# Attention with top-1 experts on one core: rows of the next sequence loaded and stored by tiles of 128 tokens, steps behind a block's end two halves later

## The chip, the core and the metric

The kernel runs on one core of a Trainium2 chip. The metric is the device time of one execution in microseconds; the time before is the median of three executions. All times below are microseconds unless a row says ns. In the profile PE is TensorE's matmuls, PEld its weight loads, DVE is VectorE, ACT ScalarE, POOL GpSimd and SP SyncE. GpSimd and SyncE each issue transfers on a queue of their own.

## What is computed

Four sequences of 2048 tokens with 512 features are normalised (layer norm), go through 16-head attention with a spectral filter on queries and keys, and through a top-1 router with eight experts of capacity 100 that share one weight matrix. Cut to what matters:

```python
xn = _layernorm(x)                                   # x: 4 x 2048 x 512
q, k, v = split(xn @ w_qkv)                          # 16 heads of 32
q, k = _spectral_filter(q, mask), _spectral_filter(k, mask)
attn = softmax(einsum('bhqd,bhkd->bhqk', q, k) / sqrt(dh))
a = einsum('bhqk,bhkd->bhqd', attn, v).reshape(B, S, D) @ w_out + b_out
f = combine @ (dispatched @ w_expert + b_expert)     # first 100 tokens of each expert
out = x + a + f
```

## The kernel before

**Tiling.** Four sequences `b`, four groups of four heads `c` in each: `k = 4 b + c` runs from 0 to 15. The queries of a group come in four blocks `n` of 512 (`QB`); a block goes over 16 key tiles of 128. Handling one key tile `j` is called a **half**, two halves are a **window**. A block has `HB` = 16 halves, a group `GH` = 64, the kernel 1024, numbered through. "Half 46 of k = 2" below is counted from that group's start.

**A half on the engines.** TensorE writes the negated row maxima into four banks of the accumulator (`negm` with `ones_b`), adds the scores (`k,q`), and between them computes scores the other way round (`q,k`) for the maxima of a later block, which VectorE reduces (`part`). ScalarE takes four exponentials into a tile called `even` or `odd`. TensorE multiplies the tile of the half before with the values, and VectorE adds the product to `num`. The accumulator `array` has eight banks, taken in turn.

**Row sums.** The tiles of a window are added by an accumulating transfer on GpSimd's queue (`even<-odd`, 1 MB, `pair`), one window later. Another window later GpSimd adds the sum of the window before to it (`add_to`, two operations of 128x1024), and waits for the transfer to land. There are five `even` tiles and three `odd` ones.

**Order.** Each engine works in program order. In each window the loop of the last lines of the kernel emits: `max_split` of a block whose maxima are complete, the entries of `heads` (a block's `divide`), the `pair` of the window before, the `add_to` of two windows before, and then for each half the matmuls and exponentials and the steps that stand in `agenda` for it. SyncE's transfers are in program order too, but an issue starts as soon as what it waits for is there, so it may run far ahead of its half.

**What ends a block.** `close_steps` (line 654) places, counted in halves from the block's end, `fold` at 5, eight `invert` at 6 to 13, `divide` in `heads` at 14 (it writes `ot` on GpSimd), four `result` (a projection of `ot` on TensorE and a copy to `y` on ScalarE) from 15 to 18, and `add` at 19: `y` is added to the output in memory, 1 MB on GpSimd's queue. So `divide` belongs to the last window of the following block. In the same window `max_split` (line 162) makes three rows of the next block's maxima on GpSimd (`rest`, `row`), and three small transfers on SyncE's queue bring them to `negm`, which the next block's first matmuls read.

**A change of sequence.** In group c = 2 of each of the first three sequences (k = 2, 6, 10) `plan` (line 862) places the first pass over the next sequence's rows: `load` of a chunk of 512 tokens (1 MB, `xs`, two buffers), `measure` (mean and variance on VectorE), `bias` (adds `b_out` on GpSimd), `first_sums` (stores the chunk to the output), `scale` (four small operations on GpSimd that turn 16 variances into factors). Then the rows are loaded again for normalising and transposing in group c = 3. The entries of `in_stage` are numbers into the tuple that `token_stage` returns: 0 load, 1 measure, 2 scale, 3 normalize, 4 turn, 5 route, 6 bias, 7 first_sums. The first sequence is measured and normalised before the loop; only its `bias` and `first_sums` are placed, in k = 0.

```python
            for n, (come, go) in enumerate(((22, 38), (30, 46), (40, 56), (48, GH))):
                at(start + come, in_stage, 0, n)
                at(start + go, in_stage, 7, n)
            for i in range(NT):
                at(start + 26 + 2 * i + 2 * (i // 8), in_stage, 1, i)
                at(start + 28 + 2 * i + 2 * (i // 8), in_stage, 6, i)
            at(start + GH - 4, in_stage, 2)
```

**Experts.** `place_experts` (line 844) gathers the experts' rows in k = 12; `gather_row`, `add_row` and `scatter_row` add them to the output in k = 13 and 14, one tile in each block.

Projections of the next group are spread over a group by `spread`, which fills halves evenly with regard to the `cost` that other steps have put there.

Of the kernel before, what the change touches and what calls it, by code (L numbers as in the profile page):

```python
# [26 lines left out]
NT = S // P  # L27
# [4 lines left out]
NQ = S // QB  # L32
TQ = QB // P
# [69 lines left out]
def attention_and_top1_experts(ctx: ExitStack, tc: tile.TileContext, a: dict, out: bass.AP):  # L103
    nc = tc.nc
    x = a["L0_attn_x"].rearrange("b (g t p) d -> b g p t d", t=TQ, p=P)
    o = out.rearrange("b (g t p) d -> b g p t d", t=TQ, p=P)
# [50 lines left out]
    def chunk(name):  # L157
        tag, bufs = ("y", 1) if name == "y" else ("xs", None)
        return chunks.tile([P, TQ, DM], F32, tag=tag, name=name, bufs=bufs)
# [25 lines left out]
    on = SimpleNamespace(sync=nc.sync)  # L185
# [36 lines left out]
    def token_stage(b):  # L222
# [4 lines left out]
        held = {}  # L227

        def load(n, tile=None):
            held[n] = chunk("xs") if tile is None else tile  # L230
            on.sync.dma_start(out=held[n], in_=x[b, n])

        def measure(i):
            on.vector.bn_stats(stats[:, i, :], held[i // TQ][:, i % TQ, :])
            on.vector.bn_aggr(mv[:, i, :], stats[:, i, :])
# [2 lines left out]
            row = held[i // TQ][:, i % TQ, :]  # L238
            on.gpsimd.tensor_tensor(row, row, b_out, ALU.add)

        def first_sums(n):

            on.sync.dma_start(out=o[b, n], in_=held[n])

        def scale(first=0, last=NT, shift_on=None):
            at = slice(first, last)
# [52 lines left out]
        first = small.tile([P, NT], F32, name="first")  # L299
# [78 lines left out]
        def enter(i):  # L378
            on.gpsimd.indirect_dma_start(
                tables[i % NTAB],  # L380
                bass.IndirectOffsetOnAxis(ap=slot[:, i : i + 1], axis=0),
                entry[:, i, :],
                None,
                bounds_check=SLOTS - 1,
                oob_is_err=False,
            )

        route = [score, by_token, below_top, exponentials, divide, best, ranked, first_best, place, carry_on, locate, note]
        route += [lambda i=i: enter(i) for i in range(NT)]
        return load, measure, scale, normalize, turn, route, bias, first_sums  # L390


    qs, ks, vs = {}, {}, {}
# [249 lines left out]
    def row_sums(tiles):  # L643
        pf = bank()
        for tile in tiles:
            four_heads(pf, lambda at: ones[:, 0:DH], tile, start=tile is tiles[0], stop=tile is tiles[-1])
        return pf

    def project(k, ot, t):
        pj = bank()  # L650
        columns(pj, ot[:, t * P : (t + 1) * P], wo[k], start=True, stop=True)
        return pj

    def close_steps(k, n):

        b = k // NG
        held = {}

        def fold():
            held["den"] = work.tile([P, QB], F32, tag="den", name="den", bufs=1)  # L660
            held["factor"] = work.tile([P, QB], F32, tag="factor", name="factor", bufs=1)
            on.scalar.copy(held["den"], row_sums([ended[k, n][1]]))

        def invert(i):
            at = slice(i * PART, (i + 1) * PART)
            on.vector.reciprocal(held["factor"][:, at], held["den"][:, at])

        def divide():
            held["ot"] = work.tile([P, QB], F32, tag="ot", name="ot", bufs=1)
            on.gpsimd.tensor_tensor(held["ot"], ended[k, n][0], held["factor"], ALU.mult)  # L670

        def result(t):
            if t == 0:
                held["y"] = chunk("y")
            on.scalar.copy(held["y"][:, t, :], project(k, held["ot"], t))

        def add():
            on.gpsimd.dma_start(out=o[b, n], in_=held["y"], accum_op=ALU.add)

        if (k, n) == (B * NG - 1, NQ - 2):  # L680
            steps = [(7, 1, fold)] + [(8 + i // 2, 0, invert, i) for i in range(QB // PART)]
            first = 12
        else:
            steps = [(5, 1, fold)] + [(6 + i, 0, invert, i) for i in range(QB // PART)]
            first = 15
        steps += [(first + t, 1, result, t) for t in range(TQ)]
        return steps + [(first + TQ - 1 + first % 2, 0, add)], (first - first % 2, divide)

    def close_last(k, n, num, tiles, y):

# [11 lines left out]
                on.sync.dma_start(out=o[b, n, :, t - 1 : t + 1, :], in_=y[:, t - 1 : t + 1, :])  # L702


    load, measure, scale, normalize, turn, first_route, first_bias, first_sums = token_stage(0)

    load(0)
    load(1)
# [8 lines left out]
    turned, filtered = ([f[2 * s + i] for f in filters for s in range(2)] for i in range(2))  # L717
# [57 lines left out]
    for i, item in enumerate(stream[:MAX_AHEAD]):  # L775
# [4 lines left out]
        half = next(turns), next(turns)  # L780
# [12 lines left out]
    HB = NT  # L793
    GH = NQ * HB
# [6 lines left out]
    def at(half, step, *args, cost=0):  # L801
        agenda[half].append(lambda: step(*args))
        costs[half] += cost
# [28 lines left out]
    def in_stage(which, *args):  # L832
        stage["all"][which](*args)
# [4 lines left out]
    def plan_route(first, step):  # L838

        costs_of = {0: NR, 1: 1, 7: 3}  # L840
        for i in range(ROUTE):
            at(first + 2 * i, step, i, cost=costs_of.get(i, 0))

    def place_experts(start):


        begin, fetch, measure, scale, expert = expert_steps()
        first = start + 36
        at(first, begin)
        for i in range(ST):  # L850
            at(first + 2 + 2 * i, fetch, i)
            at(first + 6 + 2 * i, measure, i)
        at(first + 22, scale)
        for i in range(ST + 2):
            at(first + 26 + 2 * i, expert, i, cost=(NR if i >= 2 else 0) + (1 if 1 <= i <= ST else 0))
        for i in range(ST):
            free = start + GH + i * HB + 22
            for step in (gather_row, add_row, scatter_row):
                at(free, step, i)
                free += 2  # L860

    def plan(k):

        b, c = divmod(k, NG)
        start = k * GH
        if k == 0:
            for n in range(NQ):
                at(2 + 8 * n, load, n)
                for i in range(TQ):
                    at(6 + 8 * n + i, first_bias, n * TQ + i)  # L870
                at(12 + 8 * n, first_sums, n)
        if k + 1 == B * NG:
            return
        at(start + GH // 2, load_out_weights, k + 1)
        last = start + GH - 4
        steps = []
        if k == 0:
            done = spread([(1, 0, step) for step in first_projections], 15)
            at(done[-1] + 1, load_qkv_weights, 1)
            plan_route(20, lambda i: first_route[i]())  # L880
            ready = done[-1] + 3
        if c == NG - 2 and b + 1 < B:

            at(start + 20, begin_stage, b + 1)
            for n, (come, go) in enumerate(((22, 38), (30, 46), (40, 56), (48, GH))):
                at(start + come, in_stage, 0, n)
                at(start + go, in_stage, 7, n)
            for i in range(NT):
                at(start + 26 + 2 * i + 2 * (i // 8), in_stage, 1, i)
                at(start + 28 + 2 * i + 2 * (i // 8), in_stage, 6, i)  # L890
            at(start + GH - 4, in_stage, 2)
            at(start + GH - 4, in_stage, 0, 0)
            at(start + GH + 2, in_stage, 0, 1)
        pieces = projections(k + 1)
        if c == NG - 1:

            late = {8: 9, 12: 14}
            order = [("turn", i) for i in range(8)] + pieces[:4] + [("turn", i) for i in range(8, 12)]
            order += pieces[4:8] + [("turn", i) for i in range(12, NT)] + pieces[8:]
            steps, first = [], start + 1  # L900
            for step in order:
                if isinstance(step, tuple):
                    i = step[1]
                    steps.append((1, start + late[i] if i in late else 0, lambda i=i: in_stage(4, i)))
                else:
                    steps.append((1, 0, step))
            steps[0] = (1, first, steps[0][2])
            done = spread(steps, last)
            turned = {i: done[order.index(("turn", i))] for i in range(NT)}
            for i in range(NT):  # L910
                at(turned[i] - 1, in_stage, 3, i)
            for n in (2, 3):
                at(turned[4 * n - 5] + 1, in_stage, 0, n)
            plan_route(turned[NT - 1] + 2, follow_route)
        else:
            done = spread([(1, ready if k == 0 else start, step) for step in pieces], last)
        assert done[-4] >= start + 3 * HB and done[-8] >= start + 2 * HB
        if k + 2 < B * NG:
            at(done[-1] + 1, load_qkv_weights, k + 2)
# [12 lines left out]
    for block in range(1, B * NG * NQ):  # L932

        costs[block * HB - 4] += 0.5
    place_experts((B - 1) * NG * GH)
    for k in range(B * NG):
        plan(k)
# [12 lines left out]
    for k in range(B * NG):  # L950
        for n in range(NQ):
            num = work.tile([P, QB], F32, tag="num", name="num")
            tiles = {}
            for w in range(NW):
# [9 lines left out]
                for j in (even, odd):  # L964
# [5 lines left out]
                    for u in range(2):  # L970
                        half = halves[u]
# [73 lines left out]
```

## Time and profile before

| | |
|---|---|
| Time, median of 3 (lowest, highest) | 4384.06 us (4382.21, 4387.28) |
| The profiled execution's own time | 4377.26 us |
| Its span, first to last instruction | 4375.4 us |
| Mean granted TensorE clock | 0.993 |
| GpSimd's queue (pair sums, `y`) | 605.83 MB, 70.7% of 16 engines' span |
| SyncE's queue (loads, stores, weights, `negm`) | 76.09 MB, 5.6% |
| `even` add on GpSimd, mean | 2530 ns, two for each window but the first of a block |
| `even<-odd`, issue to landing | 8.1 us median |
| `out_dram<-y`, issue to landing | 10.1 us median |

How to read it: the page lists busy time by engine, then groups of instructions as "line, engine, operation, output<-input, shapes, xcount | busy us, mean ns | idle us of its engine just before it, and what ended that idle". Nearly all instructions have line 83, that of a helper, so groups are told apart by their tiles. Other views give the waits in a stretch ("engine and tile, what it waited for: us in total, times, longest"), the busy time of each engine in stretches of time, and the instructions of an engine in order of time ("start, us, engine, line, operation, tiles, xcount [idle before <- what ended it]").

### The profile page before, as it was taken

The numbers are of one execution on the slowest core, as the hardware profiler recorded it, in microseconds if no ns is written. First come the engines' busy times: TensorE is split into PE (matmuls) and PEld (weight loads), VectorE is DVE, ScalarE is ACT, GpSimd is POOL, SyncE is SP. The second block draws the span as 40 slices with busy tenths as digits, with TensorE's granted clock in tenths as the row PEclk, the third lists the DMA queues.
The fourth block names the chain that finished last, engine by engine and source line by source line (L and its number), as shares of the span: only waits on it lengthen the run. The fifth ranks groups of instructions, "written<-read, shape, count | busy, mean of one in ns | idle before, by whom it ended". The sixth has DMA issues, their size and how long they took to land. (4 is left out here: it accounts for less than half of the span.)

```text
span 4375.4 us, 129380 instructions
## 1 busy us (share of the span) xinstructions
PE 4281.4 (98%) x56110; PEld 1906.5 (44%) x56110; DVE 3345.9 (76%) x4059; ACT 2653.9 (61%) x5527; POOL 2942.7 (67%) x2009
## 2 busy tenths in 40 slices
PE   8999999989999999999999999998999999999998
PEld 4444444434444444443544444443444443544432
DVE  6777778867777777886777877787777877677786
ACT  3556666666666666657566666665756665566665
POOL 0677666666776666776677766767668676677773
PEclk9999999999999999999999999999999999999999
DMA  4777877887777778788677777788877886778788
GB/s 116 182 140 153 158 151 164 190 186 146 141 150 154 153 152 159 168 191 184 128 156 153 154 151 154 160 173 191 165 137 153 166 165 130 142 156 162 153 158 171
DMA packets 161379, 690.71 MB, mean 158 GB/s; under 512 B 25302, under 2 KB 30584, under 8 KB 95528
## 3 DMA queue, kind: packets, MB, share of 16 engines
q0 software_dynamic: 110432, 605.83, 70.7%
q1 hardware_dynamic: 49200, 76.09, 5.6%
q8 instruction: 439, 7.19, 0.6%
q14 instruction: 132, 1.08, 0.1%
q10 hardware_dynamic: 1176, 0.52, 0.1%
HBM read 59.27 MB, written 88.96 MB: 34 GB/s over the span
## 5 line engine op out<-in xcount | busy, mean ns | idle before, releaser
L83 DVE TENSOR_REDUCE part<-array 128x2 f32<-128x1024 f32 (+1 forms) x2297 | 2427.8, 1104 | 924.4 <-PE array L83 921.0
L83 POOL TENSOR_TENSOR even<-even 128x1024 f32<-128x1024 f32 x876 | 2124.4, 2530 | 473.8 <-DMA even<-odd 473.1
L83 PE MATMUL array<-q,k 32*128 32x512 f32 x8192 | 1936.3, 593 | 0.0
L83 PE MATMUL array<-k,q 32*128 32x512 f32 x8192 | 1930.3, 591 | 2.2 <-DVE part L83 1.5
L83 ACT ACTIVATE even<-array 128x512 f32<-128x512 f32 x2048 | 1058.1, 604 | 496.0 <-PE array L83 488.2
L83 ACT ACTIVATE odd<-array 128x512 f32<-128x512 f32 x2048 | 1057.4, 603 | 485.2 <-PE array L83 387.2
L83 PEld LDWEIGHTS array<-k,q 32*128 32x128 f32 x8192 | 820.0, 187 | 423.3 <-issue 270.7
L83 POOL DMA_DIRECT2D even<-odd x510 | 468.5, 919 | 681.5 <-ACT odd L83 624.9
L83 PEld LDWEIGHTS array<-q,k 32*128 32x128 f32 x8192 | 762.5, 184 | 39.3 <-issue 17.1
L83 DVE TENSOR_TENSOR num<-num,array 128x512 f32<-128x512 f32 x960 | 649.8, 677 | 25.0 <-PE array L83 18.7
L83 PE MATMUL array<-even,v 128*32 128x512 f32 x4096 | 545.6, 605 | 14.2 <-ACT odd L83 14.2
L83 PE MATMUL array<-odd,v 128*32 128x512 f32 x4096 | 546.9, 605 | 7.4 <-ACT even L83 7.4
L83 PEld LDWEIGHTS array<-xnT,wg 128*32 128x32 f32 x15808 | 446.7, 110 | 242.5 <-issue 125.8
L83 PE MATMUL array<-xnT,wg 128*32 128x128 f32 (+1 forms) x15808 | 527.3, 277 | 0.7 <-ACT xnT L83 0.7
L83 PE MATMUL array<-negm,ones_b 3*128 3x512 bf16 x4096 | 440.7, 385 | 13.0 <-DVE num L83 7.6
L83 PEld LDWEIGHTS <-ones_b 3*128 3x128 bf16 x4096 | 111.7, 91 | 466.7 <-issue 466.7
L83 PE MATMUL array<-wo,ot 128*32 128x512 f32 x2048 | 268.9, 598 | 37.0 <-POOL ot L83 36.9
L83 PEld LDWEIGHTS array<-wg,xnT 128*32 128x32 f32 x8192 | 231.9, 110 | 124.6 <-issue 62.8
L83 DVE RECIPROCAL factor<-den 128x64 f32<-128x64 f32 x504 | 273.9, 544 | 0.0
L83 PE MATMUL array<-wg,xnT 128*32 128x128 f32 x8192 | 263.8, 273 | 0.0
L83 PEld LDWEIGHTS array<-even,v 128*32 128x32 f32 x4096 | 80.7, 108 | 408.6 <-ACT odd L83 400.4
L83 PEld LDWEIGHTS array<-odd,v 128*32 128x32 f32 x4096 | 81.0, 108 | 407.8 <-ACT even L83 398.5
(126 smaller groups left out, 1588.8 us busy)
## 6 DMA issues: line engine op xcount, KB each, us to landing
even<-odd POOLq DMA_DIRECT2D x510, 1024.0 KB, 8.1
out_dram<-y POOLq DMA_DIRECT2D x63, 1024.0 KB, 10.1
xs<-in_L_attn_x_dram SPq DMA_DIRECT2D x30, 1024.0 KB
out_dram<-xs SPq DMA_DIRECT2D x16, 1024.0 KB
wg<-wd SPq DMA_DIRECT2D x15, 768.0 KB
wo<-in_L_attn_w_out_dram SPq DMA_DIRECT2D x16, 256.0 KB
negm<-row SPq DMA_DIRECT2D x192, 4.0 KB
even<-in_L_attn_w_qkv_dram SPq DMA_DIRECT2D x2, 512.0 KB
```

The source lines that it names most:

```text
L83: done = act(*args, **kwargs)
```

## The change

Loads and stores of the first pass become transfers of 128 tokens (256 KB), with a new `load_tile`; `first_sums` takes a tile. In k = 2, 6, 10 tile i is loaded at half 20 + i + 5 (i // 4), measured three halves later, given its bias four later and stored six later; `scale` stands at half 59 and not 60; the second load of the first eight tiles is placed one tile a half from 58 on, the other eight follow tile by tile. The first sequence's rows in k = 0 are treated likewise. `result` moves from 15 to 18 to 17 to 20 halves behind a block's end, `add` from 19 to 21; `divide` stays at 14. The last closing steps (the branch with `first = 12`) stay as they are. `gather_row` and the two steps behind it move four halves. The tuple gets `load_tile` as entry 8.

```diff
+        def load_tile(i):
+            n, t = divmod(i, TQ)
+            if t == 0:
+                held[n] = chunk("xs")
+            on.sync.dma_start(out=held[n][:, t : t + 1, :], in_=x[b, n, :, t : t + 1, :])
+
...
-        def first_sums(n):
-
-            on.sync.dma_start(out=o[b, n], in_=held[n])
+        def first_sums(i):
+
+            n, t = divmod(i, TQ)
+            on.sync.dma_start(out=o[b, n, :, t : t + 1, :], in_=held[n][:, t : t + 1, :])
...
             steps = [(5, 1, fold)] + [(6 + i, 0, invert, i) for i in range(QB // PART)]
-            first = 15
+            first = 17
         steps += [(first + t, 1, result, t) for t in range(TQ)]
-        return steps + [(first + TQ - 1 + first % 2, 0, add)], (first - first % 2, divide)
+        return steps + [(first + TQ - 1 + first % 2, 0, add)], (14 if first > 14 else first, divide)
...
         for i in range(ST):
-            free = start + GH + i * HB + 22
+            free = start + GH + i * HB + 26
...
         if k == 0:
-            for n in range(NQ):
-                at(2 + 8 * n, load, n)
-                for i in range(TQ):
-                    at(6 + 8 * n + i, first_bias, n * TQ + i)
-                at(12 + 8 * n, first_sums, n)
+            for i in range(NT):
+                half = 2 + i + 5 * (i // TQ)
+                at(half, load_tile, i)
+                at(half + 4, first_bias, i)
+                at(half + 6, first_sums, i)
...
-            for n, (come, go) in enumerate(((22, 38), (30, 46), (40, 56), (48, GH))):
-                at(start + come, in_stage, 0, n)
-                at(start + go, in_stage, 7, n)
             for i in range(NT):
-                at(start + 26 + 2 * i + 2 * (i // 8), in_stage, 1, i)
-                at(start + 28 + 2 * i + 2 * (i // 8), in_stage, 6, i)
-            at(start + GH - 4, in_stage, 2)
-            at(start + GH - 4, in_stage, 0, 0)
-            at(start + GH + 2, in_stage, 0, 1)
+                half = start + 20 + i + 5 * (i // TQ)
+                at(half, in_stage, 8, i)
+                at(half + 3, in_stage, 1, i)
+                at(half + 4, in_stage, 6, i)
+                at(half + 6, in_stage, 7, i)
+            at(start + GH - 5, in_stage, 2)
+            for i in range(2 * TQ):
+                at(start + GH - 6 + i, in_stage, 8, i)
...
-            for n in (2, 3):
-                at(turned[4 * n - 5] + 1, in_stage, 0, n)
+            for i in range(2 * TQ, NT):
+                at(turned[i // TQ * TQ - TQ - 1] + 1 + i % TQ, in_stage, 8, i)
```

More of the change, by code (lines that the diff above doesn't have):

```diff
@@ L389, in token_stage @@
         route += [lambda i=i: enter(i) for i in range(NT)]
-        return load, measure, scale, normalize, turn, route, bias, first_sums
+        return load, measure, scale, normalize, turn, route, bias, first_sums, load_tile
     qs, ks, vs = {}, {}, {}
@@ L702, in close_last @@
                 on.sync.dma_start(out=o[b, n, :, t - 1 : t + 1, :], in_=y[:, t - 1 : t + 1, :])
-    load, measure, scale, normalize, turn, first_route, first_bias, first_sums = token_stage(0)
+    load, measure, scale, normalize, turn, first_route, first_bias, first_sums, load_tile = token_stage(0)
     load(0)
```

## The prediction

> **What bounds the kernel now.** I read the page first, then busy time in equal stretches, then TensorE's waits in the stretches that stand out, then the orders in time of GpSimd and TensorE there.
>
> ```profile
> span 4375.4 us, 129380 instructions
> ...
> PE 4281.4 (98%) x56110; PEld 1906.5 (44%) x56110; DVE 3345.9 (76%) x4059; ACT 2653.9 (61%) x5527; POOL 2942.7 (67%) x2009
> ...
> L83 PE MATMUL array<-wo,ot 128*32 128x512 f32 x2048 | 268.9, 598 | 37.0 <-POOL ot L83 36.9
> ```
>
> TensorE is busy for 98% of the span, and its longest idle stands before one group: the output projections `wo,ot`, which wait for GpSimd's `ot`. In stretches of 273 us TensorE lacks 0.1 to 0.4 us nearly everywhere, but 16.4, 16.3 and 15.5 us in the three that hold a change of sequence (819, 1911 and 3003 us). In stretches of 17 us (TensorE, its weight loads, DVE, ACT, GpSimd, granted clock, DMA share, GB/s):
>
> ```profile
> 887.00:904.00 17.00, 8.40 (x68) 2.71 (x64) 8.89 (x10) 5.77 (x12) 13.54 (x9) 0.86 0.66 159
> 904.00:921.00 17.00, 13.27 (x100) 4.21 (x100) 6.13 (x8) 7.65 (x14) 12.84 (x14) 0.73 0.79 200
> ```
>
> TensorE idles 12.3 us, and the clock then stands at half for some 14 us. The waits of 819 to 1092 us name it, TensorE's order in time shows where:
>
> ```profile
> PE array L83 <- POOL ot L83: 11.4, 2, 11.1
> ```
> ```profile
> 895.55 1.06 PE L83 MATMUL array<-even,v 128*32 128x512 f32 x8 [1.09 <-ACT odd L83]
> 907.73 1.93 PE L83 MATMUL array<-wo,ot 128*32 128x512 f32 x8 [11.11 <-POOL ot L83]
> 909.59 0.62 PE L83 MATMUL array<-negm,ones_b 3*128 3x512 bf16 x4
> ```
>
> Why `ot` is late, in GpSimd's order:
>
> ```profile
> 853.56 1.29 POOL L83 DMA_DIRECT2D out_dram<-y  x1
> 854.34 1.42 POOL L83 DMA_DIRECT2D even<-odd  x1
> ...
> 856.12 1.77 POOL L83 DMA_DIRECT2D even<-odd  x1
> 869.88 2.36 POOL L83 TENSOR_TENSOR even<-even 128x1024 f32<-128x1024 f32 x1 [11.99 <-DMA even<-odd]
> ```
> ```profile
> 890.78 0.87 POOL L83 DMA_DIRECT2D even<-odd  x1
> 894.94 4.66 POOL L83 TENSOR_TENSOR even<-even 128x1024 f32<-128x1024 f32 x2 [3.29 <-DMA even<-odd]
> 899.56 1.25 POOL L83 TENSOR_TENSOR xs<-xs,b_out 128x512 f32<-128x512 f32 x1
> 900.90 0.27 POOL L83 TENSOR_SCALAR rstd<-mv 128x16 f32<-128x16 f32 x1
> 901.26 2.94 POOL L83 TENSOR_TENSOR rstd<-rstd,power 128x16 f32<-128x16 f32 x1
> ...
> 904.85 0.42 POOL L83 TENSOR_TENSOR rest<-rest,row 16x128 f32<-16x128 f32 x1
> ...
> 906.42 1.25 POOL L83 TENSOR_TENSOR ot<-num,factor 128x512 f32<-128x512 f32 x1
> ```
>
> GpSimd is some 12 us behind: it waits for pair sums whose transfer queues behind the `y` store, then has biases (1.25), the scale step (900.90 to 904.85, 3.95), the split (`rest`, 1.6) and `ot` before it.
>
> **The prize.** A half has four exponentials on ACT; 64 halves of an undisturbed head group take 257.2 us (k = 4, 5, 8): 4.02 a half, blocks of 65.1, 63.9, 65.1 and 63.1 to 63.5. In k = 2, 6, 10 the last block takes 79.4, 79.4, 79.3, and block 2 is 0.7, 1.3, 2.1 over. All excess is 53 us, 17.5 a change. Of the last block's 16, 12.2 are idle (1.09 + 11.11), some 4 the half clock.
>
> **Part 1: results and `y` two halves later.** TensorE's work is only moved. A half with one extra step takes 3.92, with two 4.79; summing such lengths over the new order of TensorE's steps gives 255.8 us for a plain group on either side: nothing. `divide` stays at half 14, so `ot` may come two halves, 8 us, later. That alone would cover most of the 11.1. But what is late next is `negm`. The split stands just ahead of `ot` on GpSimd; its rows go out through SP, and the next block's first matmuls need them. In this trace the last negm transfer is issued at 906.5, the matmul comes at 909.59: 3.1 us, the least over all blocks (3.1 again in k = 6 and 10; 8.5 to 10.5 in calm blocks). Without the `ot` wait TensorE would be there at 896.6 + 1.06 = 897.7. So **the split must come 909.6 - 897.7 = 11.9 us earlier**, or its wait replaces the other.
>
> `y` (1 MB through GpSimd's queue) now follows the pair sum of window 1 and delays that of window 2. The three transfers issued from 853.56 to 856.12, down by 876.4, still take 23 us; in calm blocks GpSimd has room for either order. Nothing won or lost there; the same for the expert gathers moved four halves (behind `y` as before) and for the last block, where DMA is full (share 1.02 to 1.08 from 4310 to 4340): a wait of 4.94 there goes, but the pair sum behind `y` is later by as much; 0, ends -6 and +4.
>
> **Part 2: rows by tiles, scale one half earlier.** Biases end at half 54 instead of 60. No GpSimd work is removed (16 biases of 1.27, scale 3.95, all still ahead of the split), so only what now lies in waits is won. From 869.88 to the split: the bias at 881.1 (1.39, with the earlier issue of the pair sum 2.1) and those at 889.57 and 899.56 (2.5) go to windows where GpSimd waits for transfers; the scale step moves ahead of the add at 894.94 and fills its wait of 3.29. Sum 2.1 + 2.5 + 3.3 = 7.9. Left of 11.9: **4 us**; ends 0 (GpSimd enters the stretch less far behind) and 8 (the transfers fill the waits).
>
> Block 2 pays: by its split 12 biases are done instead of 8, and bursts of four leave GpSimd nothing (a window: 4.66 + 0.87 + 2.54 = 8.07 of 8.04). Its split ended at 828.0, the first matmul came at 831.2: already at the limit of 3.1. Half of the 2.5 us of extra biases in this block hides in its DMA wait of 11.35 (790 to 802); I take +1.5, ends 0 and 5.
>
> DVE: a half with reciprocal and measurement needs 2.36 + 0.68 + 0.55 + 0.68 + 0.18 = 4.45 of 4.02; two of four bursts of four halves fall on reciprocals, 3.4 us if nothing gives, 0.5 taken as these lie in halves of up to 4.79; ends 0 and 3.4.
>
> SP: 36 more issues a change at 0.38 us, spread over 45 halves; in order, stores wait for biases that stand ahead of the split anyway: nothing. The last negm has weights and reloads ahead of it on SP, but now such 1.7 MB, issued at 876.8 and 885.3, leave the packet record of SP's queue by 895, and the new order issues most of them some 20 us ahead: 0, ends 0 and 5.
>
> The Trainium skill speaks against the tiles: "DMA: Bandwidth & Descriptors", "Rules for kernel authors", asks for 1 MiB a transfer, and its section on the anatomy of a DMA adds 2.0 us to each. In estimate a chunk is 4.4 us in one piece and 10.4 in four. The trace: one 1 MB store was down in 4.9 us (783.3 to 788.2), another in 19.7 beside three GpSimd transfers (857.1 to 876.8). By the rule I would add 6 us to each of 12 chunks (4 loads, 4 stores, 4 reloads) of a change, 72 us of SP's queue. But each bias follows its load by four halves (16 us) and only its own tile counts, so I take 0 and let the rule widen the range.
>
> **Clock.** "TensorE: Matmul & The Clock Gate", "Part 1: The HAM clock gate", halves the clock after an idle window of 3.4 us. The rows: waits of 9.7 to 11.1 us cost 10 to 14 us at half clock, one of 4.94 (4332 to 4337) 7 us (0.83 in two stretches of 10), one of 2.68 none. A wait of 4 us is between: by the rule a drop, by the nearest row 3.4 us lost, below it none. I take 1.7.
>
> **Sum.** A change keeps 5 (the 4 us, and 1 us of lag brought over from block 2) + 1 (the late `odd` of 895.55, as now) + 1.7 + 1.5 + 0.5 = 9.7. Won: 17.5 - 9.7 = 7.8, thrice: 23.4. The profiled execution was 4377.26 (span 4375.4 and 1.9 around it), hence 4354; the median of the runs lies 6.8 above it: **4361**. The first sequence's biases (k = 0) count for nothing: TensorE waits 0.5 us there from 100 to 380.
>
> **Rivals.**
> (a) All goes: GpSimd has caught up by the split. For it: five empty halves before scale, and 8 us more for `ot`. Against: 49.6 us of DMA waits on GpSimd from 640 to 905, which no reorder of biases shortens. 4384 - 53 + 2 = 4333.
> (b) negm takes nearly all, or bursts of small transfers fill the waits in which biases are to hide: 14 to 20 stay of 17.5. 4380.
> (c) Slower: block 2's end becomes a second stall. Its split is at the limit, so each us of lag is a wait; from 4.94 up the half clock comes too. 5 + 3.4 there, 6 + 4 at the last block, 2 of `odd` and 2 of DVE: 22.4 against 17.5, thrice 15: 4399. It decides from 4 us of lag at that split.
> (d) That the edits do not act: the order of instructions shows `y`, biases and scale moved as said, so only their effect can be missing, which is (b).
>
> **Numbers.** Forecast 0.50 (own range 4349 to 4374), (a) 0.17, (b) 0.20, (c) 0.13. The range leaves out half of (a) and half of (c): 4335 to 4392. Within 0.2% (4375 to 4393), what this kernel's measurement can't tell from no change: most of (b), a little of (c), 0.20. Faster 0.68, slower 0.12.
>
> **What would show it.** The wait for `ot` gone at all three changes; a wait before `negm` matmuls of 2 to 6 us at the end of k = 2, 6, 10, and one of 0 to 3 a block earlier; scale before the add that now stands ahead of it, with less DMA wait there; a clock of 1.00 or little under; plain groups at 257.2. Wrong, if plain groups change by over 1 us, if the last block of k = 2 is at 64 (a), or if block 2 is above 70 (c).

## The result and the profile after

| | before | after |
|---|---|---|
| Median in one comparison (lowest to highest) | 4383.39 us (4382.21 to 4387.28), 4 runs | 4357.70 us (4356.41 to 4360.44), 4 runs |
| Ratio, 95% interval | 1 | 0.994 (0.9929 to 0.9952) |
| Profiled execution, span | 4377.26, 4375.4 | 4358.15, 4356.3 |

The kernel became 26 us faster; 4361 was forecast, in a range of 4335 to 4392. The page of the changed kernel, span and three of the costliest groups:

```profile
span 4356.3 us, 129604 instructions
...
L83 POOL TENSOR_TENSOR even<-even 128x1024 f32<-128x1024 f32 x876 | 2130.7, 2545 | 359.3 <-DMA even<-odd 358.3
...
L83 PE MATMUL array<-negm,ones_b 3*128 3x512 bf16 x4096 | 442.2, 386 | 32.2 <-DMA negm<-row 20.4
...
L83 PE MATMUL array<-wo,ot 128*32 128x512 f32 x2048 | 267.7, 596 | 3.1 <-POOL ot L83 3.1
```

and two of the same groups in the kernel before:

```profile
L83 POOL TENSOR_TENSOR even<-even 128x1024 f32<-128x1024 f32 x876 | 2124.4, 2530 | 473.8 <-DMA even<-odd 473.1
...
L83 PE MATMUL array<-negm,ones_b 3*128 3x512 bf16 x4096 | 440.7, 385 | 13.0 <-DVE num L83 7.6
```

The idle time that stood before `wo,ot` (37.0) is down to 3.1, and 20.4 us of waits for the small `negm` transfers have come. GpSimd's own work is as long as it was (2130.7 against 2124.4 us of additions); what shrank are its waits for the sums' transfers, from 473.1 to 358.3.

TensorE's waits in three stretches that hold the changes of sequence (800 to 1070, 1700 to 1965 and 2760 to 3025 us; total, times, longest), in three fences:

```profile
PE array L83 <- DMA negm<-row: 4.8, 2, 4.1
```
```profile
PE array L83 <- DMA negm<-row: 7.2, 2, 6.2
```
```profile
PE array L83 <- DMA negm<-row: 6.8, 2, 6.0
```

Each change has one long wait, at its end, and a short one (0.7 to 1.0) a block earlier. TensorE's order in time at the first:

```profile
895.64 1.07 PE L83 MATMUL array<-even,v 128*32 128x512 f32 x8
900.80 0.57 PE L83 MATMUL array<-negm,ones_b 3*128 3x512 bf16 x4 [4.09 <-DMA negm<-row]
```

And GpSimd's order there:

```profile
877.61 4.69 POOL L83 TENSOR_TENSOR even<-even 128x1024 f32<-128x1024 f32 x2 [6.18 <-DMA even<-odd]
882.25 0.85 POOL L83 DMA_DIRECT2D even<-odd  x1
883.24 4.66 POOL L83 TENSOR_TENSOR even<-even 128x1024 f32<-128x1024 f32 x2
887.99 0.27 POOL L83 TENSOR_SCALAR rstd<-mv 128x16 f32<-128x16 f32 x1
...
892.15 0.94 POOL L83 DMA_DIRECT2D even<-odd  x1 [0.19 <-ACT even L83]
892.85 4.94 POOL L83 TENSOR_TENSOR even<-even 128x1024 f32<-128x1024 f32 x2
897.49 0.42 POOL L83 TENSOR_TENSOR rest<-rest,row 16x128 f32<-16x128 f32 x1
...
899.06 1.25 POOL L83 TENSOR_TENSOR ot<-num,factor 128x512 f32<-128x512 f32 x1
```

The scale step (from 887.99) now precedes the addition at 892.85, which no longer waits. The split (`rest`, 897.49) still ends only when `ot` begins, 899.06; from there to the matmul that reads the rows it is 1.7 us, and TensorE, free at 896.71, stands until 900.80.

To compare kernels I use two numbers from each trace. First, the lengths of head groups, from the first exponential of one to that of the next. Second, for k = 2, 6 and 10, how long after the group's first exponential the last split starts: the mean of three. The seven plain groups are k = 1, 4, 5, 8, 9, 12 and 14. A row is one execution; the profiled ones lie between 7.4 us above the median of their kernel (rows only) and 5.7 below it (pass eight halves earlier), so differences of a few us between rows are read together with the medians. All kernels of this study:

| kernel | k = 2, 6, 10 | last split after | seven plain groups | k = 3, 7, 11 | k = 13 |
|---|---|---|---|---|---|
| before | 824.7 | 267.7 | 1802.5 | 830.6 | 294.3 |
| after | 795.7 | 259.4 | 1805.6 | 833.6 | 295.9 |
| after, once more | 796.9 | 259.8 | 1805.8 | 834.6 | 295.8 |
| results and `y` late only | 807.0 | 263.1 | 1803.0 | 833.1 | 294.8 |
| `y` late only | 811.7 | 263.5 | 1804.3 | 829.6 | 294.6 |
| rows only | 800.9 | 259.7 | 1802.2 | 831.2 | 294.9 |
| whole chunks | 810.8 | 265.1 | 1803.6 | 831.4 | 294.7 |
| scale at half 60 | 806.5 | 263.0 | 1803.7 | 834.6 | 294.8 |
| scale at half 56 | 797.9 | 260.3 | 1804.9 | 834.5 | 295.7 |
| no biases | 774.6 | 249.7 | 1805.1 | 831.9 | 295.9 |
| pass eight halves earlier | 791.9 | 259.0 | 1804.9 | 833.1 | 295.8 |
| rows and `y`, results at 15 | 794.8 | 257.8 | 1805.7 | 831.2 | 294.5 |
| the same, bias in `y` | 773.2 | 248.4 | 1805.7 | 829.8 | 294.5 |
| bias in `y`, results at 17 | 774.8 | 250.0 | 1805.1 | 832.5 | 295.7 |

(With whole chunks the stall lies in block 2 and moves the last split with it.) So the change won 29.0 us in the three groups it aimed at and gave back some 10 elsewhere: 3.1 in plain groups, 3.0 in k = 3, 7, 11, 1.6 in k = 13, and 2 at the beginning and the end. Three groups without any loss would take 3 x 257.2 = 771.6.

### The profile page after: what moved, and what is told of

Its sections match the earlier page's. It is cut to its first block, busy times and chain, and to the rows that moved or that the text cites. A ratio compares the mean times of both kernels' runs of the same rounds, so it can differ in the third digit from the quotient of the medians.

```text
span 4356.3 us, 129604 instructions
## 1 busy us (share of the span) xinstructions
PE 4286.8 (98%) x56110; PEld 1913.9 (44%) x56110; DVE 3347.1 (77%) x4066; ACT 2654.8 (61%) x5527; POOL 2946.7 (68%) x2009
## 5 line engine op out<-in xcount | busy, mean ns | idle before, releaser
L83 POOL TENSOR_TENSOR even<-even 128x1024 f32<-128x1024 f32 x876 | 2130.7, 2545 | 359.3 <-DMA even<-odd 358.3
L83 POOL DMA_DIRECT2D even<-odd x510 | 453.6, 890 | 561.9 <-ACT odd L83 468.6
L83 PE MATMUL array<-negm,ones_b 3*128 3x512 bf16 x4096 | 442.2, 386 | 32.2 <-DMA negm<-row 20.4
L83 PE MATMUL array<-wo,ot 128*32 128x512 f32 x2048 | 267.7, 596 | 3.1 <-POOL ot L83 3.1
L83 POOL DMA_DIRECT2D out_dram<-y x63 | 83.4, 1323 | 266.3 <-ACT y L83 241.2
```

Source lines behind the costliest of these rows:

```text
L83: done = act(*args, **kwargs)
```

## The experiments

Theory S is the prediction's: the time at a change is set by how late GpSimd's split comes, and GpSimd's own work counts where it does not lie in a wait for a transfer. The first four kernels ran on one chip (before: 4378.74 us there), the next four on another (4386.00), the last four on a third (4382.43), so times are compared by their ratio to before.

### Results and `y` late, rows as before

```diff
-            first = 15
+            first = 17
...
-        return steps + [(first + TQ - 1 + first % 2, 0, add)], (first - first % 2, divide)
+        return steps + [(first + TQ - 1 + first % 2, 0, add)], (14 if first > 14 else first, divide)
...
-            free = start + GH + i * HB + 22
+            free = start + GH + i * HB + 26
```

> The kernel before with only the results, `y` and the gathers moved. Theory S (what counts is when the split reaches GpSimd): the wait for `ot` goes at all three changes of sequence, and a wait for negm of 10 to 12 us stands in its place; 4376 to 4390, no change from before. Rival L (the two halves given to `ot` made the gain): waits of under 3 us at the changes, 4345 to 4362. Rival G (small transfers made the gain): no gain either, but then with `ot` still waited for or waits shorter than 10.

4363.84 us, ratio 0.997 (0.9958 to 0.9982). TensorE's order in time at the first change:

```profile
904.63 0.61 PE L83 MATMUL array<-negm,ones_b 3*128 3x512 bf16 x4 [10.03 <-DMA negm<-row]
```

The wait for `ot` went and one for `negm`, nearly as long, took its place, as S had it. But the time fell by 15 us where S said none: the last split came 4.5 us earlier.

### Rows by tiles, results and `y` as before

The diff of the run before, the other way round, on the changed kernel.

> The changed kernel with results, `y` and gathers put back to 15 and 19 halves (the rows by tiles alone). Theory S: the split comes as early as in the changed kernel, `ot` ends 2.8 us behind the split's start, so TensorE waits for `ot` 3 to 7 us at each change where it now waits 4.1 to 6.2 for negm; 4356 to 4368. Rival L: the wait of 10 to 11 for `ot` is back, 4376 to 4390.

4351.01 us, ratio 0.9936 (0.9922 to 0.995): as much as the whole change. The split came 7.9 us earlier than before, on the mean of the three changes. Since results stand at 15 here, TensorE waits for `ot`, by 6.2 us at the first change:

```profile
903.92 1.93 PE L83 MATMUL array<-wo,ot 128*32 128x512 f32 x8 [6.21 <-POOL ot L83]
905.78 0.61 PE L83 MATMUL array<-negm,ones_b 3*128 3x512 bf16 x4
```

The `negm` matmul follows at once behind `wo,ot`, which takes 1.9 us here, where plain ones take 1.1: the granted clock is 0.50 from 899.3 to 909.6. The same picture stood in the trace of before, and I shall come back to it.

### The new times with transfers of 1 MB

The first pass of k = 2, 6, 10 is shown; the rows of k = 0 and the second loads go by chunks too.

```diff
-                at(half, in_stage, 8, i)
+                if i % TQ == 0:
+                    at(half, in_stage, 0, i // TQ)
...
-                at(half + 6, in_stage, 7, i)
+                if i % TQ == TQ - 1:
+                    at(half + 6, in_stage, 7, i // TQ)
```

> The changed kernel with its new times, but rows loaded and stored in chunks of 1 MB again (load at the first tile's half, store at the last tile's). Theory S: biases, scale and split keep their places on GpSimd and only wait for transfers a little differently; waits for negm of 3 to 8 us, 4354 to 4368. Rival G: the pair sums wait behind 1 MB bursts again, waits of 10 and more at the changes, 4374 to 4390.

4363.90 us, ratio 0.9967 (0.9955 to 0.9979), 12 or so behind the changed kernel. The time is where S expected it, the place is not: the last blocks take 63.3 to 65.8, with no wait over 2.0 us, and block 2 takes 74.5 to 75.9. TensorE's order in time there, then VectorE's:

```profile
818.14 0.61 PE L83 MATMUL array<-negm,ones_b 3*128 3x512 bf16 x2 [7.28 <-DVE part L83]
```
```profile
805.96 0.55 DVE L83 RECIPROCAL factor<-den 128x64 f32<-128x64 f32 x1
816.07 0.69 DVE L83 BATCH_NORM_STATS2 stats<-xs 128x6 f32<-128x512 f32 x1 [9.56 <-DMA xs<-in_L_attn_x_dram]
816.79 0.18 DVE L83 BATCH_NORM_AGGREGATE mv<-stats 128x2 f32<-128x6 f32 x1
816.89 2.32 DVE L83 TENSOR_REDUCE part<-array 128x2 f32<-128x1024 f32 x2
```

A load of 1 MB issued at 789.4 was measured at 816.1, 27 us later. VectorE works in order: while it stands before the measurement, the maxima (`part`) behind it stand too, and so do the accumulator's banks and TensorE. In the changed kernel the first of four tiles is issued at 789.6 and measured 19 us later without a wait:

```profile
808.57 0.64 DVE L83 BATCH_NORM_STATS2 stats<-xs 128x6 f32<-128x512 f32 x1
```

Small tiles keep the load ahead of its reader.

### The scale step where it was

```diff
-            at(start + GH - 5, in_stage, 2)
+            at(start + GH - 4, in_stage, 2)
```

> The changed kernel with scale one half later (60, as before the change). Theory S with its term of 3.3 us for scale: the pair sum's add waits for its transfer again before scale, the split comes 2 to 4 us later, and so the wait for negm: 4364 to 4374. If GpSimd has no wait there for scale to fill, nothing changes: 4356 to 4361.

4364.34 us, ratio 0.9967 (0.9955 to 0.9979); the split 3.6 us later than in the changed kernel, as S had it, the `negm` waits 31.6 us in six, up to 10.3. One line of the change, half a window, is worth some 12 us. GpSimd's order in time shows the wait of 3.28 that the step fills in the changed kernel, with the step now behind it:

```profile
886.48 0.84 POOL L83 DMA_DIRECT2D even<-odd  x1
890.60 4.68 POOL L83 TENSOR_TENSOR even<-even 128x1024 f32<-128x1024 f32 x2 [3.28 <-DMA even<-odd]
895.37 0.27 POOL L83 TENSOR_SCALAR rstd<-mv 128x16 f32<-128x16 f32 x1
```

### The scale step earlier still

```diff
-            at(start + GH - 5, in_stage, 2)
+            at(start + GH - 8, in_stage, 2)
```

> The changed kernel with the scale step three halves earlier (half 56 instead of 59). Theory S: between its new place and the split GpSimd still waits for transfers, and what lies in these waits costs nothing: the split comes up to 4 us earlier, negm waits of 0 to 4 us, last blocks 64 to 68, time 4343 to 4354. Rival U: the work moved only fills one wait and the transfer behind it sets the split: within 3 us of the changed kernel (4355 to 4361).

4356.48 us, ratio 0.9935 (0.9922 to 0.9949): no gain, rival U is right here. GpSimd's order in time tells why:

```profile
881.96 0.27 POOL L83 TENSOR_SCALAR rstd<-mv 128x16 f32<-128x16 f32 x1
...
886.12 0.94 POOL L83 DMA_DIRECT2D even<-odd  x1 [0.19 <-issue]
886.82 4.93 POOL L83 TENSOR_TENSOR even<-even 128x1024 f32<-128x1024 f32 x2
891.44 1.15 POOL L83 DMA_DIRECT2D even<-odd  x1
893.98 4.66 POOL L83 TENSOR_TENSOR even<-even 128x1024 f32<-128x1024 f32 x2 [1.39 <-DMA even<-odd]
```

The step now stands ahead of a pair sum's issue, which GpSimd also makes. The transfer starts at 886.12, where the changed kernel has its issue at 882.25, and its addition waits again, by 1.39. So of the three places of the step one is best: between a transfer's issue and the addition that waits for it (half 59) it hides beside the transfer; ahead of the issue (56) it delays the transfer by its own length; behind the addition (60) the wait of 3.28 stays empty.

### No biases

```diff
-                at(half + 4, in_stage, 6, i)
```

> The changed kernel without the stage's 16 additions of b_out to the rows in k = 2, 6, 10 (b_out is left out of sequences 1 to 3). Theory S: what is left at a change (negm waits of 4.1 to 6.2 us and half the clock) is GpSimd's own work ahead of the split: 12 biases of 1.27 us stand in block 2 and the last block, so without them the negm waits at k = 2, 6, 10 are under 2 us, their last blocks take 63.5 to 66, GpSimd's waits for transfers grow; time 4336 to 4348. Rival U: the split now follows the pair sums' transfers, whatever GpSimd does between them: negm waits stay at 3 to 6 us, last blocks at 67 to 70, time 4352 to 4360.

This kernel leaves `b_out` out of sequences 1 to 3. 4333.47 us, ratio 0.9882 (0.9867 to 0.9897), 25 us under the changed kernel by the ratios (0.994 - 0.9882 = 0.0058 of 4384) and slightly below S's range. No wait of TensorE at the changes is over 1 us, the last blocks take 63.1 to 63.2, and the split comes 9.7 us earlier than in the changed kernel. So what the changed kernel still loses at a change comes from the 16 additions, 16 x 1.27 = 20.3 us of GpSimd's time.

### The first pass eight halves earlier

```diff
-            at(start + 20, begin_stage, b + 1)
+            at(start + 12, begin_stage, b + 1)
...
-                half = start + 20 + i + 5 * (i // TQ)
+                half = start + 12 + i + 5 * (i // TQ)
...
-            at(start + GH - 5, in_stage, 2)
+            at(start + GH - 13, in_stage, 2)
```

> The changed kernel with loads, measurements, biases and stores of the next sequence eight halves earlier (biases end at half 46) and scale at half 51. Theory S: the last block of a change has no stage work left on GpSimd, so its negm wait is under 2 us and the block takes 63.5 to 66; block 2, with scale and the last four biases in it, may rise from 66 to 68 and wait up to 3 us at its split; time 4336 to 4350. Rival U: last blocks stay at 67 to 70 or block 2 takes over what they lose: 4353 to 4362. Rival (c) of the prediction in its full size: block 2 above 72 and 4365 or more.

4356.97 us, ratio 0.9937 (0.9924 to 0.9951): as the changed kernel. The last blocks fall to 65.0, 64.3 and 65.4, block 2 rises to 69.7, 69.5 and 67.6. This is rival U's other half: the lag is not removed, it moves to another block's end. Block 2 had no more room, as the prediction said.

### `y` late alone, on the kernel before

```diff
-        return steps + [(first + TQ - 1 + first % 2, 0, add)], (first - first % 2, divide)
+        return steps + [(first + TQ - 1 + (3 if first == 15 else first % 2), 0, add)], (first - first % 2, divide)
...
-            free = start + GH + i * HB + 22
+            free = start + GH + i * HB + 26
```

> The kernel before with the y store alone two halves later (half 21, behind the pair sum of window 1; gathers 26), the results left at 15. Theory Y: the 15 us that late results won come from the place of y in GpSimd's queue: the split of a change 3 to 4 us earlier than before, waits for ot of 7 to 8.5 us instead of 9.7 to 11.1, last blocks 73 to 76, time 4362 to 4370. Rival R: they come from the later use of ot: here the waits for ot stay at 9.5 to 11, last blocks at 79, time 4375 to 4383. If y in the new place also costs in plain groups, they take 257.5 or more here and 257.2 in the other case.

4368.24 us, ratio 0.9962 (0.9948 to 0.9976): `y`'s place alone gives what late results and `y` gave together. The single waits for `ot`, 9.2, 11.1 and 9.2, are longer than theory Y asked for, and the second is longer than before (9.9), but before, others stood beside them: all of TensorE's idle time in the last blocks of k = 2, 6, 10 falls from 14.1, 14.2 and 14.0 to 9.3, 12.4 and 10.6. GpSimd's order in time, where the trace of before has two pair sums behind `y` and then 11.99 us of waiting:

```profile
854.69 0.84 POOL L83 DMA_DIRECT2D even<-odd  x1
855.28 1.56 POOL L83 TENSOR_TENSOR xs<-xs,b_out 128x512 f32<-128x512 f32 x1
856.50 1.61 POOL L83 DMA_DIRECT2D out_dram<-y  x1
857.28 1.74 POOL L83 DMA_DIRECT2D even<-odd  x1
862.24 4.68 POOL L83 TENSOR_TENSOR even<-even 128x1024 f32<-128x1024 f32 x2 [3.23 <-DMA even<-odd]
866.89 1.28 POOL L83 TENSOR_TENSOR xs<-xs,b_out 128x512 f32<-128x512 f32 x1
868.11 0.83 POOL L83 DMA_DIRECT2D even<-odd  x1
876.96 4.68 POOL L83 TENSOR_TENSOR even<-even 128x1024 f32<-128x1024 f32 x2 [8.02 <-DMA even<-odd]
```

One pair sum now lands ahead of `y`, so GpSimd has an addition and a bias to do (862.24 to 868.1) while `y` drains. GpSimd's waits for pair sums between 826 and 905 us fall from 21.3 us before to 17.1, and the split comes 4.2 us earlier on the mean. The other two changes show the same order: one wait of 11.95 and 11.85 us behind `y` before, two of 3.71 and 8.07, and of 3.20 and 8.51, here. No run varied how many sums land ahead of `y`.

### The changed kernel again, and three that build on it

> The changed kernel once more, for a comparison on one chip with the three that follow: ratio 0.994 to the kernel before, 4354 to 4362.

4355.74 us (4354.14 to 4360.04), ratio 0.9939 (0.9926 to 0.9953).

Rows by tiles and `y` late, results back at 15:

```diff
-            first = 17
+            first = 15
-        return steps + [(first + TQ - 1 + first % 2, 0, add)], (14 if first > 14 else first, divide)
+        return steps + [(first + TQ - 1 + (3 if first == 15 else first % 2), 0, add)], (14 if first > 14 else first, divide)
```

> The changed kernel with the results back at half 15 and y left late (21), gathers 26. Theory Y: the rows' gain and y's gain stand on different work and add up, and the results' later place only costs (0.5 us in each plain group, and GpSimd standing 5 us at the issue of y): plain groups at 257.2, waits for ot at the changes of 2 to 5 us (6.2 to 6.8 with the rows alone, 7 to 9 with y alone, 11 before), ratio 0.989 to 0.992, 4337 to 4350. Rival R: late results are what makes room for ot, without them its wait stays at 6 to 7: ratio 0.993 to 0.995, 4352 to 4362.

4348.11 us (4345.67 to 4352.01), ratio 0.992 (0.9907 to 0.9934), 7.6 us under the changed kernel of the same comparison, with no overlap of the two ranges. Waits for `ot` are 3.2 to 3.6. The split comes 9.9 us earlier than before; rows alone gave 7.9 and `y` alone 4.2, so the two gains overlap by 2. The late results are what the changed kernel pays for. GpSimd's waits over the whole run (total, times, longest), the changed kernel first:

```profile
POOL even L83 <- ACT odd L83: 468.6, 213, 13.9
...
POOL out_dram L83 <- ACT y L83: 241.2, 53, 12.2
```
```profile
POOL even L83 <- ACT odd L83: 700.3, 239, 14.0
...
POOL out_dram L83 <- ACT y L83: 11.4, 1, 11.4
```

Where results and `y` move together, GpSimd comes to the issue of `y` before ScalarE has copied it and stands there, 53 times and up to 12.2 us. That this is the cost is not shown. Nearly all of it stands in place of waits for `odd`, which fall by 231.7 us, and ahead of the first change's split only two such waits lie, of 5.1 us each and over 170 us before it. By the table, of the 8.0 us between the two profiled executions of this comparison 2.1 lie in k = 2, 6, 10, 3.4 in k = 3, 7, 11 and 1.3 in k = 13; why the later results cost time there is open. Theory Y was wrong in one point: plain groups do not go back to 257.2.

Then the bias is taken from GpSimd altogether. It is added by VectorE where results of one group in each sequence are copied out:

```diff
-                at(half + 4, first_bias, i)
...
-                at(half + 4, in_stage, 6, i)
...
+            if k % NG == (2 if b + 1 == B else 1):
+                on.vector.tensor_tensor(held["y"][:, t, :], project(k, held["ot"], t), b_out, ALU.add)
+            else:
+                on.scalar.copy(held["y"][:, t, :], project(k, held["ot"], t))
```

> As the run before, but b_out is added on DVE where the results of one head group a sequence (k = 1, 5, 9, 14) are copied out, 0.68 us each in place of ACT's copy, and GpSimd's 16 biases of 1.27 us a sequence are gone. Theory S: GpSimd's own work ahead of the split was what was left at a change, so no wait over 1 us there, plain groups 257.2 (k = 1, 5, 9, 14 up to 1.5 more where DVE gets late): ratio 0.986 to 0.988, 4322 to 4334. Rival D: DVE's 0.68 us more in the halves of the results makes TensorE wait for the maxima: k = 1, 5, 9, 14 at 261 or more and ratio 0.989 or above. Rival U (transfers set what is left): waits for ot stay at 2 us or more, 4337 or above.

4328.98 us (4326.81 to 4329.78), ratio 0.9876 (0.9861 to 0.9891): the best of the study, 1.2% under the kernel before. VectorE's group with the new operation:

```profile
L83 DVE TENSOR_TENSOR y<-array,b_out 128x512 f32<-128x512 f32 x64 | 43.9, 686 | 7.9 <-PE array L83 7.7 <-issue 0.2
```

It takes 43.9 us of an engine that is 78% busy, and k = 1, 5, 9, 14 take 258.4, 257.6, 257.6 and 257.5 against 258.6, 257.2, 257.5 and 257.8 without it: it lies in gaps. TensorE has no wait over 0.5 us at a change. With results at 17 in addition:

> As the run before with the results at half 17 as in the changed kernel. Theory Y: with nothing late at the changes the results' place costs 0.3 to 0.7 us a group: 4 to 9 us above the run before, plain groups at 257.7 to 258. Rival R: the later results give a reserve for ot that is worth as much: within 3 us of the run before, or below it.

4332.80 us (4330.61 to 4333.48), ratio 0.9886: 3.8 above. The cost is smaller than theory Y's 4 to 9 and does not lie in plain groups but in k = 2, 6, 10 (+1.6), k = 3, 7, 11 (+2.7) and k = 13 (+1.2).

## Why the prediction was right, point by point

**What bounds the kernel, and the prize.** Held. The runs without biases on GpSimd, where nothing waits at a change, bring the three groups to 773 to 775, against 771.6 that the prize of 53 us supposes (a third of it is 17.7 a change, not 17.5, which is half a microsecond in all). Rival (a), all goes at 4333, is what the run without biases took, 4333.5; the changed kernel doesn't get there because the biases are still on GpSimd.

**Results move, `negm` takes over.** Held in kind: the run with results and `y` late alone has `negm` waits of 9.7 to 10 at the changes. **The size of 3.1 us was misread.** In the trace of before the `negm` matmul stood in TensorE's order behind `wo,ot`, which waited for `ot` and ran 1.93 at half clock; it was not the transfers that took 3.1. Where nothing stands between, it is 1.7 from the split's end to the matmul (899.1 to 900.80), and so it is, between 1.69 and 1.78, in 40 of the 44 waits for `negm` over 0.4 us in the traces of this study. Block 2 was called "at the limit of 3.1" by the same misreading: there `wo,ot` (829.32) and a projection (830.20) stand between. With results at 17, `wo,ot` is gone from that place too, so TensorE is there at 896.7 and not 897.7. Corrected: the split had to come 11.9 - 1.4 + 1.0 = 11.5 us earlier, with TensorE as late as before.

**"Nothing won or lost" for `y`.** Wrong: this is the step that failed. Alone it wins 13.0 us at the three changes (4.2 us of split each). The prediction weighed the delay of the sums behind `y`, and didn't ask how many of them GpSimd has in hand to work on while `y` drains: none with `y` first, one with `y` second.

**Rows and scale, 7.9 us.** Held: rows alone bring the split 7.9 us earlier on the mean, 6.7 at the first change, where the sum was made. Its term of 3.3 for the scale step is shown by the run at half 60 (3.6); the other two, 2.1 and 2.5, were not tried apart. In the whole change the split came 8.2 earlier, as `y`'s gain overlaps with the rows'. That 4.1 us of wait stayed at the first change, where 4 were forecast, is partly luck: counted from the group's first exponential the split came 9.25 earlier there and not 7.9, but TensorE was there 1.8 earlier too, not least because the late `odd` (1.09), which the sum had kept, was gone: 11.5 + 1.8 - 9.25 = 4.05. At the other two changes the wait was 6.2 and 6.0, and in the second trace of this kernel 5.2 at the first.

**Block 2.** +1.5 and 1 of lag were forecast; block 2 takes 66.1, 66.8 and 66.2, with waits of 0.7 to 1.0, inside the 0 to 3 named; blocks 0 and 1 of these groups take 64.8. The 0.5 us put down for VectorE can't be told apart in this.

**Transfers of 256 KB.** The Trainium skill ("DMA: Bandwidth & Descriptors", "Rules for kernel authors") asks for 1 MiB where most bandwidth is wanted, which would have made the tiles the worse choice. Here the runs decide against it: with 1 MB pieces and the same times the kernel is 0.27% slower by the two ratios, and the trace shows a reader that needs a quarter waiting for the whole. The 2.0 us a transfer, which the prediction took from that page's section on the anatomy of a DMA, are stated there for transfers that GpSimd issues; the rows go through SyncE, and no run here timed a tile alone. To charge nothing for the tiles was right.

**Clock.** 1.7 was taken for a wait of 4 us, and 1.7 it was at the first change (3.4 us at half clock); at the other two, with waits of 6.2 and 6.0, it was 3.4 (6.8 us at half clock).

**What the sum left out.** Plain groups were to stay at 257.2 and take 257.7 to 258.3, and groups with routing or experts lose 1 (on the mean) and 1.6: 10 us in all, with the 2 at the two ends, which the model of unchanged sums over TensorE's steps did not show. One plain group, k = 8, went up by 1.1 us (0.8 in the second trace), just over the 1 us that the prediction had named as a sign of being wrong. The part in k = 3, 7, 11 comes with the late results: every kernel that has them takes 831.4 us or more there, every one that has not 831.2 or less. Some of it is the half clock running over the group's edge: the spell of 1959.0 to 1965.9 lies 3.2 us within k = 7. For k = 13 (294.7 to 295.9 with late results, 294.3 to 294.9 without) and for plain groups, which lie between 1802 and 1806 in all runs, it isn't settled which edit costs what.

**Why it came out near.** 23.4 was forecast for the changes and 29.0 was won; nothing was forecast elsewhere and 10 were lost. The two errors partly cancel: 4354 for the profiled execution, which took 4358.15. That the median was to lie 6.8 above the profiled time, as before, was an accident of that one execution: after, it lies 0.5 below. So 4361 against 4357.7 is near partly by errors that offset each other.

## What to carry to other kernels

On an engine that both computes and issues transfers, a step's cost depends on its place: between an issue and the work that waits for its landing the step hides beside the transfer, ahead of the issue it delays the transfer by as much. Put one transfer whose result the engine can work on ahead of a long one, and look at what stands between two events in program order before taking their distance for a transfer's time. Moving lag from one block's end to another won nothing here; taking the work off the late engine, and giving it to one with gaps, won 19 us more than the best reorder.

## What the hardware showed beside

The loss of clock goes in steps. Stretches of 3.4 us at the first change (columns: busy TensorE, weight loads, DVE, ACT, GpSimd, granted clock, DMA share, GB/s), in the kernel with rows and `y`, where TensorE idled 3.64 us:

```profile
900.50:904.00 3.50, 2.12 (x12) 0.46 (x16) 0.00 (x0) 0.12 (x1) 3.50 (x4) 0.57 0.44 116
904.00:907.50 3.50, 3.50 (x20) 1.10 (x16) 1.23 (x1) 1.55 (x3) 3.50 (x3) 0.50 1.07 250
```

and in the changed kernel, where it idled 4.09:

```profile
900.50:904.00 3.50, 3.20 (x20) 1.47 (x20) 0.84 (x1) 0.74 (x2) 3.50 (x3) 0.56 0.92 232
904.00:907.50 3.50, 3.50 (x32) 1.12 (x28) 2.54 (x4) 1.68 (x4) 2.47 (x2) 0.96 1.03 231
```

The shorter wait cost the longer spell, 6.8 us at half clock against 3.4. The Trainium skill ("TensorE: Matmul & The Clock Gate", "Part 1: The HAM clock gate") has windows of 3.4 us that run freely, one idle window halving the clock and one busy window restoring it. The traces bear out the grid: in each of the fourteen the spells begin whole multiples of 3.413 us apart and last one to four such lengths, so a shorter wait can cost more than a longer one by where it falls. They do not bear out that a whole window must be idle. In the run with the pass eight halves earlier a wait of 3.21 us, which ended at 837.55, cost 6.8 us at half clock:

```profile
833.33:836.74 3.41, 1.01 (x36) 0.74 (x28) 1.28 (x2) 0.76 (x2) 3.20 (x6) 1.00 0.03 6
836.74:840.15 3.41, 2.60 (x16) 1.45 (x20) 0.23 (x1) 0.12 (x1) 3.41 (x4) 0.50 0.85 241
```

In the kernel before, a wait of 2.68 us, which ended at 4317.54, is cut in two by the grid and cost nothing:

```profile
4312.70:4316.10 3.40, 2.15 (x17) 0.26 (x13) 1.58 (x2) 1.92 (x5) 1.30 (x1) 1.00 1.08 224
4316.10:4319.50 3.40, 1.96 (x19) 0.58 (x18) 2.20 (x4) 1.31 (x4) 0.88 (x1) 1.00 0.99 205
4319.50:4322.90 3.40, 3.31 (x32) 1.09 (x32) 3.30 (x4) 3.12 (x7) 0.00 (x0) 1.00 1.00 203
```

I laid each trace's grid over its whole run, from its first spell (97 to 104 us) on, and took TensorE's idle time in every window. Of the windows at full clock, 71 of the 72 that were idle for 1.85 us or more were followed by half clock, none of the 17208 that were idle for less than 1.66, and 2 of the 14 between. Of the windows at half clock, all 76 that were idle for 0.31 or less were followed by full clock, all 72 that were idle for 0.39 or more by another at half. The ends of matmuls are modelled in the trace, so these limits are approximate; but here about half a window of idling was enough to halve the clock, and a wait is cheapest where the grid cuts it in two.
